# Keys and values of eight wide heads computed at the outset, and urgencies set block by block

## The chip, the core and the metric

The kernel runs on one core of one Trainium2 chip. The metric is the device time of one execution in microseconds. The kernel before was timed in three runs: 1225.23, 1224.16 and 1221.81 us, median 1224.16. All views of the profile come from one further execution.

A core has five engines, each with its own queue of instructions that run in order: PE (matrix products; PEld is its loading of stationary operands), DVE (vector), ACT (activation functions), POOL (GpSimd) and SP, which here issues the DMA transfers. An instruction waits on semaphores for what it reads, and whatever is queued behind it on the same engine waits too.

## The reference, cut to what matters

Input `x` has 8 batches of 128 tokens with 256 features; `ctx` has the same shape. Everything is f32. Four transformer blocks follow one another:

- L0: norm, cross attention on `ctx` (16 heads of 16), norm, MLP (256 to 1024 to 256)
- L1: cross attention whose queries come from the result so far and whose keys and values come from both `ctx` and that result, norm, MLP
- L2: twice a norm and a *wide* cross attention on `ctx` (16 heads of 128, with one learned key and value appended), then norm, MLP
- L3: norm, self attention, norm, cross attention on `ctx`, norm, MLP

Keys and values of a wide attention depend on `ctx` and on weights alone, not on `x`:

```python
kh = (kv_in @ wk + bk).reshape(b, t, H, K)
vh = (kv_in @ wv + bv).reshape(b, t, H, K)
```

## The kernel before, in words

**Threads.** The eight batches are cut into four *threads* T0 to T3 of two batches each (`SIZES`, line 30; `Thread`, line 423). Each runs all blocks on its 256 tokens, in `blocks` (line 1301), with the names a0 (attention of L0), m0 (its MLP), a1, m1 (L1), l1 and l2 (the two wide attentions, in four *groups* of four heads each: l10 to l13, l20 to l23), m2, a4, a5, m3. T0 and T1 start at once. T2 waits until T0 has ended m1, T3 until T1 has ended m1 and T0 its wide attentions.

**What sets the order.** No order is written out by hand. `Plan` (line 80) runs while the program is built: each block is a generator that asks for operations, with an urgency. Whenever an engine is free by the planner's own costs (`_weight`, line 239), `_choose` takes the operation asked for with the lowest urgency number, then the oldest, and it is appended to that engine's queue. On the chip the queues are then fixed. The urgency is a constant for the kind of operation (norm 1.0, keys 2.0, wide keys 4.0 and so on) plus the thread's `late`, which `LATE` (line 1345) sets to one of three values per thread: front (a0 to m1), wide (l1, l2), back (m2 to m3).

**Buffers.** `Slots` count them, and a generator waits for one: 11 weight tiles of 512 KB in all and 4 per thread, 20 `kb` tiles (wide keys and queries, MLP hidden rows: an MLP takes 8), 4 `vw` tiles (wide values), 2 `bv` and one `bb` tile (value biases), 7 `t` tiles (softmax). Products of PE use PSUM banks called mm (2), tl (2) and sc (4).

**Weights.** `loader` (line 472) issues a thread's weights in the order of `weight_list`: a0, m0, a1, m1, then for each wide group k, q, v, o, and so on, each as soon as a weight tile is free. All transfers stand in SP's queue.

**A wide group** (`group`, line 1125): `keys` makes two products of w by ctx, each of 4 matmuls with 256 columns (the trace shows 8 passes), drained by ACT or DVE into four kb tiles. `queries` does the same from the normed x. `values` makes one product per batch, ctx by w with 512 columns, drained by DVE with the bias row `bv`, from which POOL has taken `bb` (`value_bias`, line 1232: two broadcast loads of 256 KB, one subtraction). Then for each batch scores, softmax, transposes, weighted values, output product. Keys and queries are asked for together; values once the keys are done.

**Narrow attentions.** a0 and a1 (`by_keys`): scores by query (sc<-k,q), DVE takes each row's maximum (mp<-sc), PE transposes it, DVE adds it to q, scores by key (sc<-q,k), ACT takes the exponential into pt, PE multiplies by v (tl<-pt,v), then DVE and ACT divide (tm, attnT) and PE makes the output product (mm<-w,attnT). a4 and a5 (`by_pairs`): eight strips per thread (four per batch), each with a multiply by the mask on DVE, an add on POOL, a minimum on DVE, four exponentials on ACT, a multiply by the reciprocal sum on POOL, and four transposes on PE (tl<-ident,t).

In the profile nearly all instructions carry line 304, that of a wrapper, so they are told apart by the tiles they write and read.

Of the kernel before, what the change touches and what calls it, by code (L numbers as in the profile page):

```python
# [18 lines left out]
P = 128  # L19
# [39 lines left out]

class Event:  # L60
# [14 lines left out]
class Plan:  # L75
# [12 lines left out]
    def __init__(self):  # L88
        self.now = 0
        self.seq = 0  # L90
        self.events = []
        self.asked = []
        self.until = {e: 0 for e in self.SEEN}
        self.weight, self.shared, self.wrote = 0, False, []
        self.both_until = {"DVE": 0, "POOL": 0}
        self.clock = Clock()
        self.log = []
        self.table = None
        self.dma_until = 0
        self.live = {}  # L100
# [76 lines left out]
    def run(self):  # L177
        self.now = max(self.until.values())
        while self.events or self.asked:
            while self.events and self.events[0][0] <= self.now:  # L180
                _, _, proc, value = heapq.heappop(self.events)
                self._step(proc, value)
            for eng in self.until:
                if self.until[eng] <= self.now:
                    got = self._choose(eng)
                    if got:
                        _, a, (_, ns, f, lat, table), load = got
                        self.asked.remove(a)
                        self.weight, self.shared, self.wrote = ns, False, []
                        if load:  # L190
                            self.weight += 1295
                            self.table = table[0]
                        value = f()
                        end = self._end(eng)
                        self.until[eng] = end
                        self.log.append((eng, self.now, end - self.now, f.__qualname__.replace("four_blocks.<locals>.", "").replace("<locals>.", "")))
                        self._later(end + (self.SEEN[eng] if lat is None else lat), a[2], value)
            at = [self.events[0][0]] if self.events else []
            at += [t for t in self.until.values() if t > self.now]
            if not at:  # L200
                break
            self.now = max(self.now, min(at))
        stuck = []
        for g in self.live.values():
            while g:
                stuck.append(f"{g.gi_code.co_name}:{g.gi_frame.f_lineno}")
                g = g.gi_yieldfrom
        assert not stuck, f"waits without end: {stuck}"


class Clock:
# [4 lines left out]
    def __init__(self):  # L216
        self.t, self.busy, self.fast = 0.0, 0.0, False
        self.end = self.W

# [9 lines left out]
    def work(self, start, ns):  # L229
        self._go(start, False)  # L230
        while ns > 1e-6:
            speed = 1.0 if self.fast else 0.5
            d = min(self.end - self.t, ns / speed)
            self._go(self.t + d, True)
            ns -= d * speed
        return self.t


def _weight(eng, name, args, kw):
# [6 lines left out]
    if eng == "PE":  # L246
        if name == "transpose":
            return 109, False
        lhsT = kw["lhsT"]
        cols = aps[0].free_size()  # L250
        if lhsT.shape[0] < P:
            return 0.539 * cols, False
        if lhsT.free_size() < P:
            return 0.494 * cols, False
        return max(224, 1.685 * cols), False
# [29 lines left out]
class Engine:  # L285
# [5 lines left out]
    def __getattr__(self, name):  # L291
        f = getattr(self._eng, name)

        def call(*args, **kw):
# [3 lines left out]
            if eng != "PE" and any(x.tensor is y.tensor and x.offset == y.offset for x in aps[1:] for y in plan.wrote):  # L298
# [4 lines left out]
            plan.shared |= both  # L303
            return f(*args, **kw)  # L304
# [21 lines left out]
def four_blocks(ctx: ExitStack, tc: tile.TileContext, a: dict, out: bass.AP):  # L326
# [40 lines left out]


# [47 lines left out]
    class Thread:  # L416
        def __init__(self, h, b0, nb):
# [10 lines left out]
            self.late = 0.0  # L428

# [42 lines left out]
    def loader(T):  # L472
        for name, shape, pieces in weight_list():
# [7 lines left out]
    def all_then(evs, then):  # L481
        for e in evs:
            yield e
        plan.set(then)
# [32 lines left out]
    def each(*rs):  # L517

        for e in [spawn(asks(r), 0.0) for r in rs]:
            yield e  # L520
# [136 lines left out]
    def product(ops, take):  # L657
# [5 lines left out]
        return spawn(taken(p, take), 0.0, Plan.SEEN["PE"])  # L663
# [6 lines left out]
    def mlp(T, name, src, e, w, b, b1, func, table, adds, to):  # L670
        hT, hT_in = yield from normed(T, src, e, w, b, adds, 2.0 + T.late)
# [22 lines left out]
        yield spawn(first(), 3.0 + T.late)  # L694
# [11 lines left out]
        yield spawn(second(), 3.0 + T.late)  # L706
# [45 lines left out]
    def attention(T, name, norm, ns, own_keys, scale, qb, kb_, vb, mask_of, masks, to):  # L752
# [7 lines left out]
        hT, hT_in = yield from normed(T, *norm, 1.0 + late)  # L760
# [8 lines left out]
        between = spawn(fill(v, 1.0 if by_key else 0.0), 2.0 + late)  # L769
# [11 lines left out]
        biases_in = spawn(cols_then(biases), 2.0 + late)  # L781
        mask_in = spawn(mask_of(mask, k, hs, ks, biases_in), 2.0 + late)
# [63 lines left out]
        k_in = [spawn(keys(s, *src), 2.0 + late) for s, src in enumerate(sources)]  # L846
        yield weight(T, f"{name}qo")
        q_in = spawn(queries(), 1.5 + late)
        v_in = [spawn(values_of(s, *src), 2.5 + late) for s, src in enumerate(sources)]
# [17 lines left out]
        yield spawn(out(), 1.0 + late)  # L867

    def by_keys(T, ns, scale, mask, masks, q, k, v, v_in, vb, attnT):
# [4 lines left out]
        def item(b, c0, n):  # L874
# [94 lines left out]
            e1 = spawn(even_part(1), 0.5 + late)  # L969
# [18 lines left out]
        for b in range(T.nb):  # L988
            for c0 in range(0, NC, 2 // ns):
                done.append(spawn(item(b, c0, 2 // ns), 0.5 + late))  # L990
# [3 lines left out]
    def by_pairs(T, ns, scale, mask, masks, q, k, v, v_in, vb, attnT):  # L994
# [4 lines left out]
        def item(b):  # L999
# [17 lines left out]
            soft = [spawn(softmax(s[:, r], b, r, mn, sm, ts), 1.0 + late) for r in range(4)]  # L1017
# [26 lines left out]
        def values(b, soft, ts, turn, next_turn):  # L1044
# [3 lines left out]
            for r in range(4):  # L1048
# [14 lines left out]
                evs.append(spawn(out_of(pt, pts[:, r]), 1.0 + late, Plan.SEEN["PE"]))  # L1063
# [23 lines left out]
        for b in range(T.nb):  # L1087
            soft, ts = yield from item(b)
            nxt = Event()
            done.append(spawn(values(b, soft, ts, turn, nxt), 0.5 + late))  # L1090
# [25 lines left out]
    def wide_attention(T, i):  # L1116
        hT, hT_in = yield from normed(
            T, T.x, 1e-5, f"L2_ln{i}_scale", f"L2_ln{i}_offset", [(T.x, T.x, f"L2_bo{i}")], 0.5)
# [6 lines left out]
    def group(T, i, hg, hT, hT_in):  # L1125

        n = f"l{i}{hg}"
        ks, qs, vs = [], [], []
        bv = new(wpool, [P, 512], "bv", bufs=2)
        bv_in = spawn(value_bias(bv, i, hg), 1.0)  # L1130
        sb = new(act, [P, 4], "sb", bufs=6)
        late, nb, nt = T.late, T.nb, T.nt
        v_in = [Event() for _ in range(nb)]

        def keys():
# [17 lines left out]
            drop(T)  # L1153
            for e in ends:
                yield e

        def queries():
            yield weight(T, n + "q")
            yield hT_in
            s = P ** -0.5  # L1160
            yield op("POOL", lambda: nc.gpsimd.tensor_scalar(
                sb, col(f"L2_bq{i}", 4 * hg, 4), s, None, ALU.mult))
            ends = []
            for m in range(0, 4, 2):
                yield (kb_slots, 2)
                two = [kb(), kb()]
                qs.extend(two)

                def take(p, two=two, m=m):
                    b = col(f"L2_bq{i}", 4 * hg + m, 2)  # L1170
                    yield from each(*(either(
                        lambda j=j: nc.scalar.activation(
                            two[j][:, :nt], p[:, j * nt : (j + 1) * nt], AF.Identity, bias=sb[:, m + j : m + j + 1], scale=s),
                        lambda j=j: nc.vector.tensor_scalar(
                            two[j][:, :nt], p[:, j * nt : (j + 1) * nt], b[:, j : j + 1], s, ALU.add, ALU.mult),
                    ) for j in range(2)))
                ends.append((yield from product(proj(T.w[n + "q"], hT, (m, m + 1)), take)))
# [29 lines left out]
        k_in, q_in = spawn(keys(), 4.0 + late), spawn(queries(), 4.0 + late)  # L1207
        yield k_in
        spawn(values(), 4.5 + late)
        yield q_in  # L1210
        ends = []
        for b in range(nb):
# [8 lines left out]
            yield spawn(asks(op("PE", products, 0)), 3.5 + late)  # L1221
            ends.append(spawn(after_scores(T, i, hg, b, s, vs, v_in[b], n), 0.0 + late, Plan.SEEN["PE"]))
# [78 lines left out]
    def blocks(T):  # L1301
# [3 lines left out]
        if h > 2:  # L1305
            yield wide_done[h - 3]
        spawn(loader(T), 0)
        T.late = LATE[h][0]
# [3 lines left out]
            lambda *to: key_bias(*to, "mask_b", U8, T, True), 0, x)  # L1312
        yield from mlp(T, "m0", x, 1e-5, "L0_ln2_w", "L0_ln2_b", "L0_fc_b", AF.Gelu_apprx_tanh, GELU_T,
                       [(x, x, "L0_proj_b")], x)
        yield (x1_slots, 1)
        x1 = new(act, [P, nb, D], "x1", bufs=2)
        yield from attention(
            T, "a1", (x, None, None, None, [(x1, x, "L1_out_b"), (x, x, "L1_mlp_b2")]), 2, False, 0.0625,
            lambda m, n=1: col("L1_q_b", m, n), lambda m, n=1: col("L1_k_b", m, n), col("L1_v_b", 0, NC),
            lambda *to: key_bias(*to, "mask_i", I32, T, False), 0, x1)  # L1320
        yield from mlp(T, "m1", x1, 1e-6, "L1_postnorm_w", None, "L1_mlp_b1", AF.Gelu_apprx_tanh, GELU_T,
# [3 lines left out]
        T.late = LATE[h][1]  # L1325
        for i in (1, 2):
            yield from wide_attention(T, i)
        plan.set(wide_done[h])
        T.late = LATE[h][2]
        yield from mlp(T, "m2", x, 1e-5, "L2_ln_mlp_scale", "L2_ln_mlp_offset", "L2_b_fc1", AF.Gelu, GELU,  # L1330
                       [(x, x, "L2_b_fc2")], x)
        yield from attention(
            T, "a4", (x, 1e-5, "L3_ln1_s", "L3_ln1_b", [(x, x, "L3_b_ao")]), 1, True, 0.25,
            lambda m, n=1: col("L3_b_qkv", m, n), lambda m: col("L3_b_qkv", 2 + m), col("L3_b_qkv", 4, NC),
            lambda t, *_: score_mask(t, a["mask_s"]), 1, x)
        yield from attention(
            T, "a5", (x, 1e-5, "L3_ln2_s", "L3_ln2_b", [(x, x, "L3_b_co")]), 1, False, 0.25,
            lambda m, n=1: col("L3_b_q", m, n), lambda m: col("L3_b_kv", m), col("L3_b_kv", 2, NC),
            lambda t, *_: score_mask(t, a["mask_x"][T.batches]), nb, x)
        yield from mlp(T, "m3", x, 1e-5, "L3_ln3_s", "L3_ln3_b", "L3_b1", AF.Gelu_apprx_tanh, GELU_T,  # L1340
# [4 lines left out]


    LATE = [(0.0, 0.0, 2.3), (3.0, 0.1, 4.5), (2.3, 1.3, 2.6), (1.3, 0.8, 2.3)]

    def inputs():
        for T in threads:  # L1350
# [12 lines left out]
            yield 2000 if h == 0 else 8000  # L1363
    spawn(inputs(), 0)
# [44 lines left out]
```

## Time and profile before

| | |
|---|---|
| the profiled execution | 1224.51 us |
| its span (first to last instruction) | 1222.7 us |
| mean granted TensorE clock | 0.975 |
| PE waits from 0 to 61 us, longest | 8.3 (first weights), 4.7 (row maxima on DVE) |
| PE waits from 61 to 153 us, longest | 1.7 (row maxima on DVE) |
| PE waits from 1131 us on, longest | 6.6 (a strip on POOL), 4.3 (a strip's sum on DVE) |
| DMA, mean over the span | 118 GB/s; 296 in the first 30.6 us |

A row of the timeline gives the start in us, the duration in us, the engine, the line, the operation, output<-inputs, the shape and the count of instructions, and in brackets the idle time before it and what ended it. In the table by stretches a row gives its bounds and length, the busy us of PE, PEld, DVE, ACT and POOL with their instruction counts, and then the granted clock, the mean busy share of the DMA engines and GB/s. In the page's strip of 40 slices (30.6 us each) a digit is a tenth.

### The profile page before, as it was taken

The page shows a single profiled execution, that of the slowest core. Times are in us where ns is not written, and L with a number is a line of the kernel's source. Part 1 is how long each engine was busy: PE and PEld are TensorE (multiplying, and loading weights), DVE is VectorE, ACT ScalarE, POOL GpSimd, SP SyncE. Part 2 cuts the span into 40 slices and gives each one's busy share as a digit, 9 for nine tenths or more (in the row PEclk, how much of TensorE's full clock was granted, in tenths as well). Part 3 has the DMA queues.
Part 4 walks back from the last instruction along what each step waited for, and adds up shares of the span by engine and source line. Part 5 has one row for each costly group of instructions (what it writes and reads, how often), then busy time and mean ns, then how long its engine had stood idle before and what let it go on. Part 6 is the DMA issues. An engine that isn't in the chain of part 4 may idle for free.

```text
span 1222.7 us, 21753 instructions
## 1 busy us (share of the span) xinstructions
PE 1146.0 (94%) x8224; PEld 936.9 (77%) x8224; DVE 759.8 (62%) x1955; ACT 563.1 (46%) x1418; POOL 341.9 (28%) x397
## 2 busy tenths in 40 slices
PE   6699799999999999999999999999999999989868
PEld 4577577787877877868877888888887888877647
DVE  6665668625773546758668564444637756788771
ACT  4244445344533334527346443335333634968652
POOL 3021111111112212116424120221212522676660
PEclk9699899999999999999999999999999999989879
DMA  9133142444434443553434325454436245321400
GB/s 296 42 92 106 36 130 90 138 123 138 118 120 140 146 150 101 147 171 99 121 92 136 106 91 187 141 159 139 143 121 179 75 149 156 111 81 44 131 1 18
DMA packets 107320, 145.57 MB, mean 119 GB/s; under 512 B 6736, under 2 KB 66256, under 8 KB 107216
## 3 DMA queue, kind: packets, MB, share of 16 engines
q1 hardware_dynamic: 107216, 144.18, 38.4%
q8 instruction: 65, 1.06, 0.3%
q14 instruction: 39, 0.32, 0.1%
HBM read 143.11 MB, written 1.05 MB: 118 GB/s over the span
## 4 chain that ended last, share of the span: by engine, by line
PE 78%; DVE 11%; ACT 6%; DMA 3%; issue 1%; POOL 1%; SPq 0%; ACTq 0%; DVEq 0%; POOLq 0%
PE mm L304 56%; PE tl L304 17%; PE sc L304 5%; DVE t L304 1%; ACT t L304 1%; ACT L304 1%; DVE mp L304 1%; DVE rz L304 1%; DMA w<-in_L_k_w 1%; DVE q L304 1%; DVE tm L304 1%; ACT pt L304 1%; DVE mn L304 1%; DVE x L304 1%; ACT q L304 1%
## 5 line engine op out<-in xcount | busy, mean ns | idle before, releaser
L304 PE MATMUL mm<-hT,w 128*128 128x256 f32 x1216 | 289.8, 385 | 9.3 <-ACT kb L304 2.0
L304 PEld LDWEIGHTS mm<-hT,w 128*128 128x128 f32 x1216 | 226.7, 192 | 47.5 <-issue 5.9
L304 POOL TENSOR_TENSOR t<-t,sm 128x512 f32<-128x512 f32 x128 | 131.8, 1043 | 337.9 <-DVE sm L304 206.5
L304 PE MATMUL mm<-ctxT,w 128*128 128x256 f32 x608 | 145.4, 384 | 9.6 <-DMA w<-in_L_k_w 9.5
L304 PE MATMUL mm<-w,ctxT 128*128 128x512 f32 (+1 forms) x352 | 144.0, 539 | 1.9 <-ACT kb L304 0.9
L304 PEld LDWEIGHTS mm<-ctxT,w 128*128 128x128 f32 x608 | 113.0, 192 | 26.7 <-issue 9.8
L304 DVE TENSOR_TENSOR x<-mm,x 128x256 f32<-128x256 f32 (+1 forms) x96 | 49.0, 510 | 131.2 <-PE mm L304 130.9
L304 POOL TENSOR_TENSOR x<-x,row 128x512 f32<-128x512 f32 x40 | 50.8, 1270 | 272.3 <-ACT xn L304 180.4
L304 PE MATMUL mm<-w,at 128*128 128x256 f32 x512 | 121.5, 381 | 1.3 <-PE mm L304 1.0
L304 PE MATMUL mm<-w,kb 128*128 128x256 f32 x512 | 117.8, 380 | 0.0
L304 PEld LDWEIGHTS mm<-w,at 128*128 128x128 f32 x512 | 95.0, 190 | 19.0 <-issue 3.7
L304 PEld LDWEIGHTS mm<-w,kb 128*128 128x128 f32 x512 | 95.5, 190 | 14.1 <-issue 1.4
L304 ACT ACTIVATE t<-t,mn 128x128 f32<-128x128 f32 x256 | 99.0, 391 | 8.4 <-DVE mn L304 6.5
L304 PE MATMUL tl<-ident,t 128*128 128x128 f32 x512 | 79.9, 287 | 16.6 <-POOL t L304 9.8
L304 PEld LDWEIGHTS mm<-w,ctxT 128*128 128x128 f32 x352 | 63.4, 192 | 39.3 <-issue 32.1
L304 POOL TENSOR_TENSOR t<-t,mask 128x512 f32<-128x512 f32 x64 | 80.4, 1280 | 46.3 <-DVE t L304 44.2
L304 PEld LDWEIGHTS tl<-ident,t 128*128 128x128 f32 x512 | 63.3, 147 | 34.2 <-POOL t L304 18.7
L304 ACT ACTIVATE t<-t 128x516 f32<-128x516 f32 x64 | 40.5, 633 | 101.9 <-DVE t L304 101.8
L304 ACT ACTIVATE kb<-mm,cols 128x256 f32<-128x256 f32 x128 | 53.2, 471 | 71.2 <-PE mm L304 70.9
L304 ACT ACTIVATE at<-tl,cols 128x128 f32<-128x128 f32 x204 | 58.2, 368 | 54.8 <-PE tl L304 54.5
L304 POOL TENSOR_TENSOR bv<-bv,bb 128x512 f32<-128x512 f32 x32 | 40.6, 1270 | 115.2 <-DMA bb<-in_L_bias_v 94.6
L304 DVE TENSOR_SCALAR kb<-mm,cols 128x256 f32<-128x256 f32 x61 | 28.9, 481 | 66.6 <-ACT kb L304 64.8
(117 smaller groups left out, 1798.6 us busy)
## 6 DMA issues: line engine op xcount, KB each, us to landing
w<-in_L_wk SPq DMA_DIRECT2D x32, 512.0 KB, 4.3
w<-in_L_wq SPq DMA_DIRECT2D x32, 512.0 KB, 3.7
w<-in_L_wv SPq DMA_DIRECT2D x32, 512.0 KB, 3.7
w<-in_L_wo SPq DMA_DIRECT2D x32, 512.0 KB, 3.4
w<-in_L_mlp_w SPq DMA_DIRECT2D x16, 512.0 KB, 3.9
bv<-in_L_bv SPq DMA_DIRECT2D x32, 256.0 KB, 4.6
bb<-in_L_bias_v SPq DMA_DIRECT2D x32, 256.0 KB, 5.7
w<-in_L_w_fc SPq DMA_DIRECT2D x16, 512.0 KB, 3.9
```

What stands on the lines that cost most here:

```text
L304: return f(*args, **kw)
```

## The change

`keys_values` is cut out of `group`: the keys, the values and the loading of their bias row, as they were. `group` uses what has been made ahead, or calls it. `AHEAD` names l10 and l11 for T0: in `blocks`, before a0, T0 calls `keys_values` for these two groups, with urgency 3.49 (keys) and 4.5 (values) plus 1.5 plus 2.88. `loader` issues their k and v weights right behind those of a0. The tiles made then (8 kb, 4 vw) are held until the groups l10 and l11 use them.

All urgencies come from a table `U`, and `LATE` has ten values per thread, one for each block, in the order a0, m0, a1, m1, l1, l2, m2, a4, a5, m3.

The rest is in the planner alone: one cost (1.7 for 1.685 ns per column), a count in its log, a comparison of tiles by name, and a filler for an idle PE that is used only if `WARM` is true.

```diff
+WARM = False
+AHEAD = [[(1,0),(1,1)], [], [], []]
+U = {'take': 0.14, 'taken': -0.72, 'norm': 0.36, 'mask': 1.76, 'k': 2.41, 'q': 2.06, 'v': 2.5, 'by key': 0.2, 'softmax': 1.76, 'weights': -0.92, 'pairs': 0.3, 'out': 0.79, 'mlp norm': 0.29, 'mlp 1': 3.6, 'mlp 2': 2.57, 'wide norm': -1, 'wide k': 3.49, 'wide q': 4.0, 'wide v': 4.5, 'wide s': 0.97, 'wide': -0.64, 'ahead': 1.5}
+LATE = [(2.88, 1.56, 0.04, -1, 1.83, -0.14, 2.53, 0.98, 4.06, 2.81), (7.76, 5.97, 5.95, 4.01, 0.47, 2.2, 4.82, 1.78, 8.24, 10.19), (2.78, 0.96, 1.14, 1.19, 2.28, -0.66, 4.81, 2.47, 1.97, -1), (0.03, 1.64, 0.89, 1.66, 0.47, 1.11, -0.31, 0.16, 0.6, -1)]
...
-        return max(224, 1.685 * cols), False
+        return max(225, 1.7 * cols), False
...
     def loader(T):
-        for name, shape, pieces in weight_list():
+        names = list(weight_list())
+        first = {f"l{i}{hg}{x}" for i, hg in AHEAD[T.h] for x in "kv"}
+        ahead = [x for x in names if x[0] in first]
+        names = [x for x in names if x[0] not in first]
+        for name, shape, pieces in names[:2] + ahead + names[2:]:
...
-    def group(T, i, hg, hT, hT_in):
+    def keys_values(T, i, hg, step_back):
 
         n = f"l{i}{hg}"
-        ks, qs, vs = [], [], []
+        ks, vs = [], []
         bv = new(wpool, [P, 512], "bv", bufs=2)
-        bv_in = spawn(value_bias(bv, i, hg), 1.0)
-        sb = new(act, [P, 4], "sb", bufs=6)
-        late, nb, nt = T.late, T.nb, T.nt
+        bv_in = spawn(value_bias(bv, i, hg), U["mask"] + step_back)
+        nb, nt = T.nb, T.nt
         v_in = [Event() for _ in range(nb)]
...
+        k_in = spawn(keys(), U["wide k"] + step_back)
+        spawn(all_then([k_in], None, lambda: spawn(values(), U["wide v"] + step_back)), 0)
+        return ks, vs, k_in, v_in
...
-        k_in, q_in = spawn(keys(), 4.0 + late), spawn(queries(), 4.0 + late)
+        q_in = spawn(queries(), U["wide q"] + late)
+        ks, vs, k_in, v_in = T.ahead.pop((i, hg), None) or keys_values(T, i, hg, late)
         yield k_in
-        spawn(values(), 4.5 + late)
         yield q_in
...
         spawn(loader(T), 0)
+        for i, hg in AHEAD[h]:
+            T.ahead[i, hg] = keys_values(T, i, hg, LATE[h][0] + U["ahead"])
         T.late = LATE[h][0]
...
-    LATE = [(0.0, 0.0, 2.3), (3.0, 0.1, 4.5), (2.3, 1.3, 2.6), (1.3, 0.8, 2.3)]
```

## The prediction, made before the changed kernel ran

> **What bounds the kernel now.** I read the page first, then the table of busy time by stretches of 3.4 us, the timeline of TensorE at both ends, and its waits by stage.
>
> ```profile
> span 1222.7 us, 21753 instructions
> PE 1146.0 (94%) x8224; PEld 936.9 (77%) x8224; DVE 759.8 (62%) x1955; ACT 563.1 (46%) x1418; POOL 341.9 (28%) x397
> ...
> PE   6699799999999999999999999999999999989868
> ...
> PEclk9699899999999999999999999999999999989879
> ```
>
> TensorE is the bound, but a busy share says nothing of pace. So I price each row of PE's order by its pace start to start where PE waits for nothing: 1.73 us for one product (8 passes of 256 columns, 1199.55 to 1201.28 in the third fence), 0.44 us for four transposes, 1.10 for 32 score passes, 1.01 for 32 passes of pt by v, 0.87 for 8 passes of 128. All rows of PE's order sum to 1090 us, and the changed kernel's order has the same rows in the same shapes: also 1090. What can change is the other 133 us of the span, the **lead** (time minus PE work done so far). Where it grows: T0's m0 starts at 62.53 with 27.0 us of work behind it, a lead of 35.5; T3's a4 scores start at 1101.88 with 1004.8, a lead of 97.1; the end has 133. So the first 62 us cost 35, the last 121 us cost 36, and 1040 us between cost 62, mostly in small steps (PE waits 11 us in 214 to 1039).
>
> The start, by PE's timeline:
>
> ```profile
> 27.75 0.85 PE L304 MATMUL tl<-ident,mp 128*128 128x128 f32 x4
> 31.07 2.09 PE L304 MATMUL sc<-q,k 32*128 32x128 f32 x32 [2.47 <-DVE q L304]
> 35.14 1.94 PE L304 MATMUL tl<-pt,v 128*32 128x128 f32 x32 [1.99 <-ACT pt L304]
> 37.01 2.09 PE L304 MATMUL sc<-q,k 32*128 32x128 f32 x32
> 41.10 1.94 PE L304 MATMUL tl<-pt,v 128*32 128x128 f32 x32 [2.00 <-ACT pt L304]
> 42.97 1.96 PE L304 MATMUL sc<-k,q 32*128 32x128 f32 x32
> 49.62 2.09 PE L304 MATMUL sc<-k,q 32*128 32x128 f32 x32 [4.70 <-DVE mp L304]
> 51.64 3.58 PE L304 MATMUL mm<-w,attnT 128*128 128x256 f32 x8
> ```
>
> PE has nothing but the two first attentions, each a chain PE, DVE, PE, ACT; it waits, and what it does takes twice its pace (2.09 for 1.10).
>
> The end:
>
> ```profile
> 1164.81 1.17 PE L304 MATMUL sc<-k,q 32*128 32x128 f32 x32
> 1172.59 2.11 PE L304 MATMUL tl<-ident,t 128*128 128x128 f32 x8 [6.61 <-POOL t L304]
> 1178.96 1.08 PE L304 MATMUL tl<-ident,t 128*128 128x128 f32 x4 [4.25 <-DVE sm L304]
> ...
> 1192.70 1.89 PE L304 MATMUL mm<-w,attnT 128*128 128x256 f32 x8
> ...
> 1199.06 0.66 PE L304 MATMUL tl<-ident,xn 128*128 128x128 f32 x4 [1.01 <-ACT xn L304]
> 1199.55 1.89 PE L304 MATMUL mm<-w,kb 128*128 128x256 f32 x8
> 1201.28 1.89 PE L304 MATMUL mm<-hT,w 128*128 128x256 f32 x8
> ```
>
> T3's last attention (a5) sends eight softmax strips through POOL (add 1.28, multiply 1.04 each: 18.6 us) between its scores and its output product at 1192.70, with too little other work on PE.
>
> **The change, part by part.**
>
> *Keys and values ahead.* Eight rows of PE's order, 1.73 us each, 13.8 us in all, go from behind T0's m1 (in before 167 us and later) into T0's and T1's a0. If they only fill waits, they are free there and missing later, where PE hardly waits: at most 13.8 off, plus what the clock gives.
>
> What they bring along is not free. In SP's order two bv transfers (256 KB each) now stand ahead of T0's first weights: 0.52 MB at 296 GB/s is 1.7 us, so the first product goes from 8.30 to about 10. Then the two bb loads: there is one bb buffer, so the second waits on SP for POOL's subtraction of the first (1.27 us), and behind it on SP stand T1's mask, x, context and all its weights. Bytes ahead of the end of the first bb: 3.7 MB, 12.4 us, from about 3 us: it lands near 16; POOL then has T0's row sum (1.27) and the subtraction: SP is free near 18.5. T1's mask, issued at 6.65 before, lands near 21.4. In DVE's order T1's nine mask instructions (17.62 to 19.76 before, 2.1 us) stand ahead of T0's last q drain. So that drain ends near 24 (20.3 before), and T0's first scores near 25 (21.5). With T1's norm and key drains between the two maxima (2.35 each), the key-side scores start near 35.0 where before they started at 31.07. From there PE has filler: wide keys and values stand in each of the gaps shown, and at full pace two scores and two pt-by-v rows save about 4 us. DVE then sets the pace: the tails of both items (3 to 4 us each), four value drains (about 0.6), T1's maxima. I get T0's a0 output product near 55 (51.64 before) and T0's m0 near 65 (62.53), now with 40.8 us of PE work behind it: lead 24 instead of 35.5, **11 us off**. Ends: 15 if SP's wait costs nothing (transfers land as before), 5 if T1's chain, now 4 us later, holds T0's by DVE at each turn.
>
> The clock, which is part of this:
>
> ```profile
> 27.30:30.72 3.42, 1.27 (x7) 0.67 (x5) 2.28 (x4) 1.13 (x2) 0.00 (x0) 1.00 1.10 352
> 30.72:34.13 3.41, 2.09 (x32) 1.82 (x32) 0.80 (x2) 0.92 (x1) 0.00 (x0) 0.54 0.46 160
> 34.13:37.54 3.41, 2.40 (x40) 1.93 (x44) 0.00 (x0) 1.36 (x2) 0.00 (x0) 0.50 0.00 0
> ```
>
> The stretch from 27.30 has PE busy 1.27 of 3.42 (granted clock, third column from the end, 1.00); after it the clock is near 0.5, and stays so at 2.40 of 3.41. The Trainium skill ("TensorE: Matmul & The Clock Gate", section "HAM oscillation — how this bites in real kernels") gives as abstract rule that gaps over some 3.4 us of idle PE must be avoided. The longest gap before this fall is 2.47 us (28.60 to 31.07), so the row says that short gaps with a low busy share suffice (the page's next section, on psum-queue depth-cycling, tells of such a case). By the rule, closing the 4.70 us gap alone would keep the pace; by the row it takes a high share throughout. My walk has PE dense from 26 to 50 us, so both give full pace there; but between 50 and 65 it has two gaps of about 3 us, and by the rule they are free, by the row they cost one or two stretches at half pace, 2 us. I take the row; it is in the 65.
>
> *Held buffers.* Eight of 20 kb buffers and all four vw buffers are held from the outset until T0's first wide groups. T0's and T1's m0 need eight kb each; both orders run them one after the other, so nothing is late: 0. If the cover fails, one m0 waits a drain (0.5 us).
>
> *The middle: urgencies by block.* T1's a1 and m1 move back by some 45 us of PE work, T0's wide groups forward. The filler that left (13.8 us) was used from 167 to 214, where DVE is near 90% busy but PE waits only 3 us; in its place stand T0's groups 2 and 3, and T1's DVE-heavy a1 is spread out. Counting PE work between producer and consumer in both orders: of 64 scores-to-transposes distances 15 are under 8 us before and 14 after; of 36 from a block's output to its norm's transposes 18 and 15 are under 6. So the middle is about as well covered: −1 for one half of a maximum (1.2 us) that now stands behind T0's m1 norm on DVE, where PE stood still around 140. Ends −6 and +6: a tenth of the lead of 62 either way.
>
> *The end.* The chain is T3's: a4 scores, a4 output, a5 scores, a5 output, end; before 37.9, 19.8, 33.2 and 30.0, together 120.8. After: T2's a4 is finished ahead of T3's a4 scores, so POOL has there T3's 18.6 and one foreign add (19.8), in place of two foreign adds, a row sum and small ones beside the 18.6 (23.7) and a backlog of some 3 us: 31. Output to a5 scores as before: 19. a5 has the same POOL order; PE has 17.4 us of other work (T2's m3) in place of 11.1, so less half pace: 31. At the end m3 of T3 stands alone, with 21.2 us of rows in place of 24.7: plus the 1.0 wait shown, 1.2 for the uncovered hT drain, 4 for the last sum and store: 27.5. Sum 108.5. T3's a4 scores stand 2.3 us of PE work further back: 120.8 − 108.5 − 2.3 = **10 off**. Ends 3 (a4 no shorter, only the last two terms) and 15 (T3's m2 to a4, where PE waited 3.4, covered too).
>
> The costs in the planner (1.7 for 1.685 per column), the count in the log and the idle filler (off: WARM is False) issue nothing: 0.
>
> Sum against the profiled execution (span 1222.7, 1224.51 in all, 0.3 above the median of 1224.16): 1224.5 − 11 − 1 − 10 = **1202**.
>
> **Rivals.** Differences within 0.3% (3.7 us) are what a measurement here can't tell from none.
> - *The start is held by SP's queue* (chance 0.15): T1's data late by more than 4 us and T0's chain held behind it on DVE and PE in turn; start −3. For: 0.9 DMA share in the first 30 us, DVE full at 17 to 27. Against: filler needs neither. 1224.5 − 3 − 1 − 10 = 1211.
> - *The end is as long as ever* (0.10): the eight strips are fixed, and T2's a5 strips fall on T3's a4. Start −11, end 0: 1213.
> - *Both ends give all* (0.08): −15 and −15, middle −3: 1192.
> - *Slower* (0.07): the filler is missed. From 177 to 211 DVE is about 0.9 busy; if it reaches 1.0 there, because T0's groups 2 and 3 come earlier with their own softmaxes, the 13.8 us reappear as PE waits in that place, plus about 3 of half pace; with no gain at the end: 1224.5 − 11 + 17 − 1 = 1229. It decides when PE waits over 15 us between 150 and 230.
> - That the change doesn't do what it says is excluded: the eight rows stand in PE's order between T0's q product and a0 output.
>
> The likeliest case has 0.60 and its own range 1194 to 1211. The range 1188 to 1218 leaves out the slower case, part of the end's and the edges: 2 in 10. Faster 0.87, within 0.3% 0.06, slower 0.07.
>
> **What would show it.** First product near 10; a gap on SP before T1's mask; granted clock 1.0 from 27 to 50; T0's m0 near 65; between 62 and 1100 the lead grows by 55 to 68; T3's a4 scores to the end in about 108 us, m3 alone at the end. Wrong if m0 of T0 starts after 70, if PE waits over 15 us between 150 and 230, or if T3's a4 takes 38 us again.

## The result, and the profile after it

The changed kernel takes 1217.96 us (median of 7 runs, 1215.24 to 1219.29) where the kernel before, run beside it, takes 1221.81 (1220.25 to 1226.0): a ratio of 0.9955, 95% interval 0.9939 to 0.9971. That is 0.45% faster, 5.5 us on 1221.81, where 22 us were forecast. The time is just inside the upper edge of the stated range (1218). The profiled execution has a span of 1217.5 us, 5.2 under that of before.

The page of the changed kernel, the same rows as before:

```profile
span 1217.5 us, 21717 instructions
PE 1141.4 (94%) x8224; PEld 932.9 (77%) x8224; DVE 761.1 (63%) x1950; ACT 558.1 (46%) x1402; POOL 340.6 (28%) x394
...
PE   4888887999999999999999999999999999998878
...
PEclk9989988999999999999999999999999999999989
```

TensorE's busy time is about the same, so its work is done at other times, with waits in other places. The first slice, where the change put work, has fallen from 6 to 4 and the second risen from 6 to 8; the third to seventh (61 to 214 us) read 88887 where they read 99799: the moved work has left there. At the far end the clock reads 9989 for 9879. PE's timeline at the start:

```profile
11.38 3.75 PE L329 MATMUL mm<-ctxT,w 128*128 128x256 f32 x8 [11.38 <-DMA w<-in_L_k_w]
...
27.48 0.81 PE L329 MATMUL sc<-k,q 32*128 32x128 f32 x8 [5.36 <-DVE q L329]
28.21 6.10 PE L329 MATMUL mm<-ctxT,w 128*128 128x256 f32 x16
34.24 1.17 PE L329 MATMUL sc<-k,q 32*128 32x128 f32 x32
...
40.26 1.17 PE L329 MATMUL sc<-q,k 32*128 32x128 f32 x32
```

The filler does what it was meant for from 34 us on: 32 score passes take 1.17 us and no wait stands between them, where before they took about 2 from 31 to 51 us. But PE stood still for 5.36 us ahead of 27.48, and the 16 passes after it took 6.10 us in place of 3.5: the granted clock was 0.84, 0.50 and 0.66 in the three stretches from 23.9 to 34.1. The last two of them:

```profile
27.30:30.72 3.42, 3.25 (x14) 2.60 (x15) 3.38 (x10) 1.39 (x4) 0.44 (x2) 0.50 1.05 355
30.72:34.13 3.41, 3.41 (x11) 2.57 (x10) 2.16 (x11) 1.78 (x4) 0.00 (x0) 0.66 1.05 348
```

PE waited for T0's last q drain on DVE, which stands behind T1's mask:

```profile
24.76 0.29 DVE L329 TENSOR_SCALAR mask<-mask 128x256 f32<-128x256 uint8 x1 [6.12 <-DMA mask<-in_mask_b]
...
26.80 0.53 DVE L329 TENSOR_SCALAR q<-mm,par,qs 128x256 f32<-128x256 f32 x1
```

The rows of SP's issues show why the mask was late:

```profile
8.43 0.96 SPq L415 DMA_DIRECT2D row<-in_rows  x1
10.50 9.05 SPq L415 DMA_DIRECT2D bb<-in_L_bias_v  x2
19.59 0.43 SPq L415 DMA_DIRECT2D mask<-in_mask_b  x1
20.06 0.43 SPq L415 DMA_DIRECT2D x<-in_x  x1
```

Two bb loads take 9.05 us to issue, since the second waits for POOL's subtraction of the first, which in this kernel ends at 19.18:

```profile
17.91 1.27 POOL L329 TENSOR_TENSOR bv<-bv,bb 128x512 f32<-128x512 f32 x1
```

T1's mask is issued at 19.59, and everything of T1 follows it. In the kernel before it was issued at 6.65:

```profile
6.65 0.92 SPq L383 DMA_DIRECT2D mask<-in_mask_b  x1
```

The DMA view of the first 30 us, 40 slices of 0.75 us:

```profile
DMA  0003799988999999996310000005676699999999
GB/s 0 0 15 66 183 328 361 281 183 232 305 285 355 371 381 382 384 380 225 124 41 25 5 11 0 0 16 186 145 181 239 244 284 352 380 386 350 374 386 337
```

The engines moved almost nothing from about 15 to 20 us. The Trainium skill ("DMA: Bandwidth & Descriptors", section "Anatomy of one DMA — SWDGE (gpsimd) path") says that a wait for a semaphore is done by the issuing sequencer and never by the DMA engines; the page says it of transfers issued by GpSimd, and these two views agree for SP: while SP waits in its queue, the transfers behind it are not issued and the engines run dry.

The end of PE's timeline:

```profile
1169.20 0.68 PE L329 MATMUL tl<-ident,t 128*128 128x128 f32 x4 [3.31 <-POOL t L329]
...
1191.05 1.89 PE L329 MATMUL mm<-w,attnT 128*128 128x256 f32 x8
...
1199.21 7.32 PE L329 MATMUL mm<-hT,w 128*128 128x256 f32 x32 [0.66 <-ACT hT L329]
1206.37 7.07 PE L329 MATMUL mm<-w,kb 128*128 128x256 f32 x32
```

T3's a4 scores start at 1108.33, its a4 output product at 1138.76, its a5 scores at 1157.25, its a5 output at 1191.05; m3 stands alone after it. From the a4 scores to the end it is 109.2 us (120.8 before).

### The profile page after: what moved, and what is told of

It is laid out like the page before. It is cut to its first block, busy times and chain, and to the rows that moved or that the text cites. A ratio compares the mean times of both kernels' runs of the same rounds, so it can differ in the third digit from the quotient of the medians.

```text
span 1217.5 us, 21717 instructions
## 1 busy us (share of the span) xinstructions
PE 1141.4 (94%) x8224; PEld 932.9 (77%) x8224; DVE 761.1 (63%) x1950; ACT 558.1 (46%) x1402; POOL 340.6 (28%) x394
## 4 chain that ended last, share of the span: by engine, by line
PE 78%; DVE 12%; ACT 6%; DMA 2%; issue 1%; POOL 0%; SPq 0%; ACTq 0%; DVEq 0%; POOLq 0%
PE mm L329 56%; PE tl L329 17%; PE sc L329 5%; DVE tm L329 2%; ACT t L329 2%; DVE t L329 1%; DVE rz L329 1%; DVE mp L329 1%; DVE q L329 1%; ACT L329 1%; ACT q L329 1%; DMA w<-in_L_wo 1%; DMA w<-in_L_k_w 1%; DVE mx L329 1%; DVE ry L329 1%
## 5 line engine op out<-in xcount | busy, mean ns | idle before, releaser
L329 PE MATMUL mm<-ctxT,w 128*128 128x256 f32 x608 | 148.8, 389 | 13.3 <-DMA w<-in_L_k_w 11.4
L329 PE MATMUL tl<-ident,t 128*128 128x128 f32 x512 | 75.7, 279 | 11.3 <-POOL t L329 5.7
L329 PEld LDWEIGHTS tl<-ident,t 128*128 128x128 f32 x512 | 60.6, 143 | 27.7 <-POOL t L329 10.4
L329 PEld LDWEIGHTS tl<-kb,kb 128*128 128x128 f32 x512 | 63.5, 192 | 12.3 <-issue 6.9
L329 ACT ACTIVATE kb<-mm,sb 128x256 f32<-128x256 f32 x67 | 30.9, 472 | 90.4 <-PE mm L329 88.1
```

## Experiments

All compare with the kernel before, run on the same chip beside them. "Lead" is the prediction's: the time less the PE work done so far.

### The planner left free: four versions of the change

My first theory was: the end comes from the urgencies alone; the start lost its gain to SP's queue; 6 to 7 us were lost around 190 us, where the filler was taken from.

**noahead**, `AHEAD = [[], [], [], []]`, the urgencies and the planner's new cost alone:

> The changed kernel with no group ahead: l10 and l11 stay where they were, the new urgencies remain. Theory (the end's 9 us come from the urgencies alone; the moved keys and values gain 2 us at the outset and lose 6 to 7 between 62 and 214 us, where they were the filler): T0's m0 starts with a lead of about 35.5 us again, T0's l10 q products with about 53, a4's scores to the end of the span stay 109 us; time 1211 to 1215. Rival (the loss between 62 and 214 us is the new urgencies' own, the move is a gain): the lead at T0's l10 q products stays near 60, the start loses its 2 us, time 1219 to 1223.

**one**, `AHEAD = [[(1,0)], [], [], []]`:

> Only l10's keys and values ahead, l11's back in T0's wide block: the outset issues one load into bb instead of two, so SP does not wait for POOL, and half of the filler is back at 176 to 194 us. Theory (SP's stop at the second bb delays T1's mask, whose VectorE preparation stands ahead of T0's last q drain): T1's mask lands by 21 us instead of 24.8, the 5.4 us stop of PE ahead of T0's scores shrinks below 2, T0's m0 starts with a lead of 26 to 30 instead of 33.4; with half the loss at 176 to 194 us gone, time 1207 to 1213. Rival (the start is held by VectorE's order and the clock, not by SP): lead at m0 33 to 36, since there is less work to put there; time 1215 to 1220.

**late**, in `value_bias` for these two groups:

```diff
+        if T.h == 0 and (i, hg) in AHEAD[0]:
+            yield ctx_in[1]
         yield (bv_slots, 1)
```

> Both groups ahead as in the changed kernel, but their two bias loads (bv and bb) are issued only when T1's inputs are in. Theory (the SP queue holds the start): the first weights go out ahead of the biases, T1's mask lands by 20 us, the 5.4 us stop ahead of T0's scores goes, T0's m0 starts with a lead of 25 to 28; the loss at 176 to 194 us stays; time 1209 to 1213. Rival (the start is held elsewhere): lead at m0 stays 32 to 35 and time 1216 to 1220; or the values, now waiting for their bias, come too late to fill, and the lead at m0 is above 35.

**aheadold**, the change's `AHEAD` with the urgencies and late values of before (U: take 0, taken 0, norm 1, mask 2, k 2, q 1.5 ...):

> l10 and l11 ahead, but with the urgencies and late values of the kernel before: the move alone. Theory (the end comes from the urgencies alone, the move gains 2 at the outset and gives back 6 to 7): a4's scores of T3 to the end of the span take 118 to 121 us again, time 1224 to 1230, slower than before. Rival (part of the end's gain is the move's, which takes work out of the middle and lets the threads end closer): the end takes 109 to 114 us and time is 1215 to 1221.

| | median | ratio | span, profiled |
|---|---|---|---|
| noahead | 1232.28 | 1.0060 (1.0037 to 1.0083) | 1233.0 |
| one | 1232.34 | 1.0063 (1.0043 to 1.0083) | 1233.3 |
| late | 1235.78 | 1.0091 (1.0074 to 1.0109) | 1233.5 |
| aheadold | 1269.60 | 1.0355 (1.0325 to 1.0386) | 1264.2 |

Every one is slower than the kernel before. Neither theory nor rival had that for noahead, one and late, and aheadold is 40 us beyond the worst that was expected. At the outset late did what was said: T0's m0 starts with a lead of 26.2 us where the changed kernel has 33.4. What differs is the far end. The page and one of PE's waits in noahead:

```profile
PE   6699899999999999999999999999999999979956
```

```profile
1210.17 1.11 PE L329 MATMUL tl<-ident,xn 128*128 128x128 f32 x4 [4.46 <-ACT xn L329]
```

The last four slices are 9956. Laid on the trace, PE's order has T3's m2 at about 1104 us in noahead (1067 in the changed kernel), and T2 finished by about 1151 (1198): T3's chain is left alone. The planner picks by urgency what is ready at the moment; a change at the outset can change every choice behind it, and the urgencies that gave a short end in the changed kernel's order gave a long one in these. So the theory of the end fell as put: from 1000 us to the end of the span the lead grows by 36 us in the changed kernel, by 47 in the kernel before, and with the changed kernel's urgencies by 57 in noahead and 56 in one and in late. (aheadold grows by 66 there and is already 17 us behind the changed kernel at 1000.) Such versions cannot tell what the move costs.

### The order held fixed

So I wrote the changed kernel's order down, each engine's list of operations and the order in which each kind of buffer is granted, and had the planner follow it. An operation whose key starts with one of FREE is outside the list and is taken when the next listed one is not ready:

```diff
+        want = SCRIPT[eng][self.at[eng]] if SCRIPT and self.at[eng] < len(SCRIPT[eng]) else None
+        there = SCRIPT and any(zlib.crc32(a[4].encode()) == want and any(o[0] == eng for o in a[3]) for a in self.asked)
         for a in self.asked:
+            if SCRIPT and zlib.crc32(a[4].encode()) != want and (there and eng != "SP" or not a[4].startswith(FREE)):
+                continue
```

Now one thing moves at a time. In the traces a_late and a_late2 have exactly the changed kernel's instructions in its order on PE, DVE and ACT; their lists differ on SP and POOL alone, by the bias loads and subtractions. a_qfirst differs in its one exchange on DVE.

**a_minus**: `AHEAD` empty, FREE holds l10's and l11's keys, values, biases, and the weight loads (the others keep their order, but T0's m0 weights come ahead of T1's inputs again, as in the kernel before).

> The four runs before let the planner make a new order each time, and every one ended differently (the third thread done by 1151 to 1157 us instead of 1198, the fourth alone after that), so they do not show the move by itself. Here the changed kernel's order is written down, every engine's list of operations and every grant of a buffer, and replayed; only l10's and l11's weights, biases, products and evictions are taken out of it and put where the planner asks for them without the move, as filler when the next listed operation is not ready. All else stands as in the changed kernel: the move undone under the new order. Theory M (the filler's absence costs what was lost between 62 and 214 us, 6.6 us, and the move gains 2 at the outset): 1211 to 1215. Theory Z (work placed earlier is only borrowed; PE's missing time up to 200 us is set by the first thread's chain of waits, and was 59 us in both orders): 1216 to 1220, a lead of 34 to 36 us at T0's m0 and of 58 to 60 us at 200 us. Rival (the move is a gain, the new urgencies lost in the middle): 1221 to 1227.

**b_plus**: the list of the kernel before, `AHEAD` as in the change, FREE holds the same keys, values, biases and weights.

> The mirror of a_minus: the order of the kernel before written down and replayed, with only l10's and l11's weights, biases, products and evictions taken out and put at the outset as in the change. The move alone under the old urgencies' order; the end stands as before (120.8 us from a4's scores of T3). Theory Z: 1220 to 1225, no difference. Theory M: the time before plus 4, 1224 to 1230. Rival (the move gains what the prediction gave it): 1209 to 1214.

**a_one**: as a_minus, `AHEAD = [[(1, 0)], [], [], []]`, FREE holds only l11's.

> The changed kernel's order replayed with l10 ahead as it is and only l11's weights, bias, products and evictions put back into T0's first wide block. One bb load is left at the outset, so SP does not wait there, and half of the filler is back at 176 to 194 us. Theory Z: 1216 to 1220 whatever the start does. Theory that SP's queue and the missing filler each cost: lead at T0's m0 28 to 31 instead of 33.4, time 1208 to 1213.

**a_late**: the changed kernel's list, FREE holds the two biases, `value_bias` waits for `ctx_in[1]`.

> The changed kernel's order replayed, with one thing moved: the loads of bv and bb for l10 and l11 stand behind T1's inputs in SP's queue (their POOL subtractions follow them); PE, VectorE and ScalarE have exactly the changed kernel's lists. Theory on the start: T1's mask lands by 20 us instead of 24.8, T0's last q drain ends by 23, the lead at T0's m0 is 26 to 29 instead of 33.4. Whether that is kept: by theory Z it is lost again by 200 us (lead 57 to 60, time 1215 to 1219); by its rival it stays, 1210 to 1213.

**a_bias**: as a_minus, but the biases stay in the list, at the outset (`first = set()` in `loader`).

> As a_minus (changed kernel's order, l10's and l11's weights, products and evictions back in T0's first wide block), but with the loads of their two biases and POOL's two subtractions left at the outset, where the change puts them: the suspected cost alone, without any of the moved PE work. Theory on SP's queue (two bv loads ahead of T0's first weights, and a second bb load that waits for POOL with everything of T1 behind it): the lead at T0's m0 rises from a_minus's 34.3 us to 39 to 41, time 1218 to 1221. Rival (the move costs through PE's own products and the missing filler): lead 34 to 36, time 1213 to 1216, as a_minus.

**a_qfirst**: the changed kernel's list, entries 8 (T1's mask) and 9 (T0's last q drain) of VectorE exchanged.

> The changed kernel's order replayed with one exchange on VectorE: T0's last q drain goes ahead of the nine instructions on T1's mask. SP's queue stays as in the change, so T1's mask still lands at 24.8 us. Theory (the late mask costs by way of VectorE's order, since T0's q drain stands behind it): T0's second score passes start at 20 to 22 us instead of 27.5, T0's m0 begins with a lead of 28 to 30 instead of 33.5, time 1213 to 1215, most of what a_late gained. Rival (T1's own start is what counts, its mask, x, context and weights all wait behind bb): T0 comes earlier, but the lead at T0's l10 q products stays 57 to 59 and the time 1216 to 1219.

**a_late2**: as a_late, and l11's bias waits for its own value weights:

```diff
+        if "T0/l11" in plan.cur:
+            yield weight(threads[0], "l11v")
```

> As a_late, but l11's two bias loads stand behind l11's weights too. In a_late PE stopped 3.9 us at 34 us for l11's key weights, which stood in SP's queue behind the second bb load. Theory: this stop goes too, lead at T0's m0 25 to 26 instead of 29.1, time 1209 to 1212. Rival (the stop is DMA bandwidth, the 0.5 MB of weights land no earlier): unchanged, 1212 to 1215.

**a_onelate**: a_one with l10's bias behind `ctx_in[1]`.

> As a_one (only l10 ahead), with its bias loads behind T1's inputs. In a_one one bv load stands ahead of T0's first weights, and the first product begins at 9.13 us instead of a_late's 7.59. Theory: 1 to 1.5 us better than a_one, 1209.5 to 1211, by a first product at 7.6 to 8.2. Rival (T0's normed input sets the start, not its weights): as a_one, 1211 to 1213.

| | median | ratio (interval) | T0's m0 starts | lead there | lead at T0's l10 q | span |
|---|---|---|---|---|---|---|
| before | | 1 | 62.53 | 35.5 | 57.5 | 1222.7 |
| the change | 1217.96 | 0.9955 (0.9939 to 0.9971) | 74.19 | 33.4 | 60.1 | 1217.5 |
| a_minus | 1214.01 | 0.9919 (0.9903 to 0.9936) | 61.22 | 34.2 | 57.6 | 1212.2 |
| a_bias | 1221.17 | 0.9984 (0.9974 to 0.9993) | 68.28 | 41.3 | 66.9 | 1219.5 |
| a_qfirst | 1217.08 | 0.9955 (0.9938 to 0.9971) | 72.53 | 31.7 | 58.4 | 1217.4 |
| a_late | 1213.35 | 0.9914 (0.9895 to 0.9932) | 69.83 | 29.0 | 53.8 | 1210.6 |
| a_late2 | 1206.26 | 0.9864 (0.9849 to 0.9879) | 63.75 | 22.9 | 47.8 | 1205.2 |
| a_one | 1211.28 | 0.9897 (0.9878 to 0.9915) | 60.43 | 26.5 | 53.0 | 1207.5 |
| a_onelate | 1210.40 | 0.9900 (0.9886 to 0.9915) | 60.78 | 26.9 | 53.7 | 1208.0 |
| b_plus | 1250.18 | 1.0210 (1.0188 to 1.0233) | | | | 1246.3 |

PE has done 27.0 us of work at T0's m0 in before, a_minus and a_bias, 33.9 with one group ahead, 40.8 with two. Spans and leads are of one profiled execution each; that of the change was the slowest of its seven runs.

Against what was expected: the times of a_minus and a_one came in the ranges of their theories, a_bias a fraction of a us beyond (41.3 and 1221.17), a_late just above its rival's, a_onelate in its theory's, but no better than a_one by the ratios. a_late2 gained more than its theory had, a_qfirst nothing, and b_plus lost far more than any of its three.

What follows, one by one:

- **a_minus: the move, as made, costs 4 us; the rest of the change gains 10** (1214.01 beside 1223.97 for before). Its interval and the change's do not overlap. Of the two theories M is right in the number. Z, that work placed early is only borrowed, falls with a_late2 as well.
- **a_bias: the cost is the bias loads on SP.** With no PE work moved, they alone add 7.2 us to a_minus (1214.01 to 1221.17; 8 by the two ratios), and 7.1 to the lead at m0. SP's row is that of the change:

```profile
10.40 9.03 SPq L789 DMA_DIRECT2D bb<-in_L_bias_v  x2
19.47 0.43 SPq L789 DMA_DIRECT2D mask<-in_mask_b  x1
```

- **a_qfirst: not by the place of T0's q drain alone.** The 5.36 us stop moved; the time did not (0.9955 both). In its place PE has a stop of 3.38 us, and T0's row maxima on DVE are hardly earlier:

```profile
27.05 2.86 PE L750 MATMUL mm<-ctxT,w 128*128 128x256 f32 x8 [3.38 <-DVE kb L750]
...
27.98 2.35 DVE L750 TENSOR_REDUCE mp<-sc 128x8 f32<-128x1024 f32 x2
```

The wide keys' drain stands behind T1's mask on DVE in turn, and the maxima stand behind T1's mask and norm: they start at 27.98 (29.10 in the change, 20.44 in a_late2). So DVE's order does pass T1's lateness on to T0, at more than one place. The expected 1213 to 1215 was wrong, its rival right.

- **a_late and a_late2: freed of this, the move gains 12.6 us at the start (lead 22.9 for 35.5).** The prediction gave it 11 with SP's wait counted in, and 15 without. a_late came to 29.0, not half the way there from the change's 33.4: behind its second bb load stood l11's key weights, and PE waited 3.9 us for them at 34 us. In a_late2 each bias stands behind what PE needs first:

```profile
20.30 3.72 PE L750 MATMUL mm<-ctxT,w 128*128 128x256 f32 x16
23.95 1.17 PE L750 MATMUL sc<-k,q 32*128 32x128 f32 x32
...
29.97 1.17 PE L750 MATMUL sc<-q,k 32*128 32x128 f32 x32
...
63.75 4.24 PE L750 MATMUL mm<-hT,w 128*128 128x256 f32 x16
```

```profile
6.57 0.70 SPq L837 DMA_DIRECT2D mask<-in_mask_b  x1
...
19.10 0.34 SPq L837 DMA_DIRECT2D bb<-in_L_bias_v  x1
```

PE never stops between 20 and 46 us, the clock is 1.00 from 13.65 us, where its records begin, to 51.2, and m0 starts at 63.75 with a lead of 22.9: 11.3 under a_minus. It is the best kernel here, 1.4% under before (ratio 0.9864) and 0.9% under the change by the two ratios. Two things moved with the biases, the bv loads that stood ahead of T0's first weights (first product at 8.00 for 11.38) and the wait for the second bb; how the gain is shared between them was not tried.

- **The filler is missed, for 4 to 6 us.** At the end of the span a_late2's 11.3 have become 7.0, and the change's 0.8 has become −5.3. Nearly all of this is lost by 214 us: after 150 us of PE work the lead is 58.2 in a_minus, 63.2 in the change and 50.9 in a_late2, and from there on the three differ by nearly the same to the end. Between 150 and 230 us PE waits 13.0 us in the change, 9.1 in a_late2, 4.4 in a_minus and 3.7 in before. I had read the 5.87 us stop at 189.68 as the missing filler. In a_minus, where the filler is back, the same row waits almost as long:

```profile
177.19 0.63 PE L699 MATMUL tl<-ident,xn 128*128 128x128 f32 x4 [4.36 <-DVE tm L699]
```

The waits that a_minus doesn't have stand on both sides of this row. One of the change's:

```profile
211.94 1.16 PE L329 MATMUL tl<-kb,kb 128*128 128x128 f32 x8 [1.35 <-DVE q L329]
```

- **One group or two.** One group ahead has a single bb load, so SP doesn't wait, and it has 7.7 of the 11.3. Here the bias's place is nearly free (a_onelate, 0.9900 to 0.9897: no difference; the first product comes 0.7 earlier, and the lead at m0 is no smaller), which speaks for the wait, not the bytes of the bias loads, as the larger cost with two groups.
- **b_plus is no measure of the move.** The planner put all eight products ahead of T0's first scores, and there they stand on the chip:

```profile
45.75 0.50 PE L747 MATMUL sc<-k,q 32*128 32x128 f32 x8
```

T0's first scores start at 45.75, 26 us later than before (20.01), and the time is 26 us longer (1250.18 against 1223.97; 23.6 by the spans): the delay reached the end nearly in full, though 13.8 us of moved work were done meanwhile. The move under the old urgencies, well placed, was not tried.

## Why the prediction was wrong, point by point

The three terms were −11 (start), −1 (middle), −10 (end). Read as lead they came out as −2, +6 and −9; the span changed by −5.2. Two steps failed: what the bias loads do to the start, and a middle said to be as well covered without the filler.

- **The end: right.** Predicted 108.5 us from T3's a4 scores, measured 109.2; as lead, from there to the end 26.7 after 36.0, −9.3 where −10 was put. Its four terms, 31, 19, 31 and 27.5, measured 30.4, 18.5, 33.8 and 26.4: a5 was to be 2 us shorter and wasn't, and the other three made up for it. a_minus and a_late2 take 108.9 for the same stretch, so it is not the move's doing. With the order held and the move undone (a_minus) the span is 10.5 under before while the lead at T0's l10 q is the same (57.6 and 57.5). So the gain of the rest of the change lies behind. That it was the urgencies as such was too much: noahead has them and a longer end. It is the order that they gave in the changed kernel. The planner's new cost went with them; that it does nothing, as the prediction had it, was not tried apart.
- **The middle failed too: "about as well covered: −1".** From T0's m0 to T3's a4 scores the lead grows by 67 us in the change, by 61 before and in a_minus: +6, and it is the move's. From 214 us on there is no difference (37.6, and 38.0 before), so all of it lies ahead, where the filler had been. The prediction saw that PE waited only 3 us there, and took T0's groups 2 and 3 for as good a cover. PE's waits between 150 and 230 are 13.0 us (3.7 before): the sign named for the slower case, over 15, was nearly met. The filler's absence costs 4.3 us (a_late2 against a_minus) to 6.1 (the change against a_minus); the place and the returned waits fit, though what ends each of them was not tested.
- **The start failed: "11 us off".** Its step was what the moved groups bring along: "it lands near 16 ... SP is free near 18.5. T1's mask ... lands near 21.4 ... So that drain ends near 24". Measured: SP free at 19.59, the mask in use at 24.76, the drain's end at 27.33, first product 11.38 for 10. Each link was named and each was a little short, 1.1 to 3.4 us. The key-side scores then start at 40.26, where 35.0 was put; with the biases behind (a_late2) they start at 29.97. So the prediction had them 3.9 us later than before (31.07), and they came 9.2 later. The larger mistake was to follow only the mask. All of T1 stood behind the same wait: x, context and weights are issued 9 to 12 us later than before (T1's x at 20.06, 8.18 before), and the planner's order interleaves T0 and T1 on VectorE and PE. The prediction put T1's chain at "4 us later", with 5 off if that held T0's by DVE; T1's key drain on DVE starts 10.2 us later (34.43, 24.19 before). a_qfirst shows that clearing T0's drain alone does not help while T1 is late. Measured by a_bias, the biases' place costs 7.2 us by itself; by a_late2 against the change (spans 1205.2 and 1217.5) it costs 12.3, 11 by the ratios. A second, smaller error is not SP's: from the key-side scores to T0's m0 the prediction put 30 us, and it is 33.9 in the change and 33.8 in a_late2, though the two gaps of about 3 us that it had there are 4.19 and 2.06 in both. Which of its terms was short there stays open.
- **The rival "start held by SP's queue"** (0.15) was the case. Its 1211 was still too low, since it charged nothing for the filler: it kept 3 us of gain at the start, 2.1 were measured, but the move as a whole came to +5.3 (spans 1217.5 and 1212.2).
- **The clock: the row was right, not the rule.** The change's stop of 5.36 us, which both would punish, was followed by two stretches at 0.50 and 0.66. In a_late2 a stretch from 58.02, with PE busy 1.42 of 3.41 us and no gap over 2.06, was followed by one at 0.50:

```profile
58.02:61.43 3.41, 1.42 (x36) 1.22 (x36) 2.23 (x12) 2.75 (x3) 0.60 (x1) 1.00 0.73 84
61.43:64.85 3.42, 3.42 (x38) 2.73 (x37) 3.07 (x7) 1.67 (x3) 2.41 (x6) 0.50 0.26 43
```

By the rule on gaps over some 3.4 us it would have been free; by the row it costs one stretch at half pace, as priced.

Put together from the spans: −10.5 for the order of the rest (a_minus), −11.3 for the filled start and +4.3 lost again later (a_late2 against a_minus), and +12.3 for the biases' place in SP's queue make −5.2. The sum closes because each term is the difference of two neighbours; the runs of one kernel spread over 1.6 us (a_minus) to about 6 (before), so each term is good to a few us.

## What to carry to other kernels

Work that is moved ahead brings its loads with it, and a load that waits for a buffer holds every load behind it on the issuing engine: list what stands behind it, all of it, and put the waiting load last. When a planner orders the work, a version with one option changed can be another order throughout: with the order made anew, no group, one group and late biases were 14, 14 and 18 us slower than the change; with the order held, the same three were 4, 7 and 5 faster. To learn what one part costs, hold the order fixed and move that part alone. A gain that is read from the first stage can be lost in part where the moved work had been a cover, even if PE hardly waited there.

## What was not expected of the hardware

- With SP in its wait, the DMA engines fell from 384 GB/s to under 30 for some 4 us, and the mask, first behind it, then took 5.2 us from its issue at 19.59 to its use at 24.76.
- The first product of a_late2, from 8.00 us, takes 3.75 us for 8 passes, half the later pace (1.89), and so do those of before and of the change. The views give a granted clock of 1.00 there, but the trace's clock records begin only at 13.65 us (13.94 in before, 15.99 in the change), so this 1.00 is no reading. What limits the first product was not tried.
